# Mixing, gating and FFN pieces of a two-layer WKV/MoE kernel, put in another order on one core

## The chip, the cores and the metric

One NeuronCore of a Trainium2 chip runs the whole program; all tensors are float32. The metric is the device time of one execution in microseconds (us). The kernel before took 5168.45 us, the median of three runs (5164.87 to 5170.24). Durations below come from one profiled execution of it.

## The reference, cut to what matters

B = 4 batches, T = 1024 tokens, C = 1024 channels. `x` and the side input `f` are both (4, 1024, 1024). A bidirectional recurrence ("mixing") is run twice with other constants, for layer 0 and layer 1, on the same `f`:

```python
ek, ekv = exp(min(f, 30)), exp(min(f, 30)) * f
nf, df  = forward scans of ekv, ek along T;   nb, db = backward scans
euk     = exp(min(u + f, 30))
num, den = nf + nb - ekv + euk * f, df + db - ek + euk
mixed   = sigmoid(x) * num / max(den, 1e-8) * (0.8 + 0.2 * tf)

x = x + mixed_L0(x) @ (weight * scale[:, None]).T + bias      # layer 0
c = mixed_L1(x)                                               # layer 1, gated by the new x
x = x + moe(rmsnorm(c) * norm_w) + c     # router, top 4 of 32 experts, and a shared FFN
```

So layer 1's scans need nothing of layer 0's result; only its gate, `sigmoid(x)`, does.

## The kernel before, in words

Channels lie on the 128 partitions, eight channel tiles `ct`, and time runs along the free axis. Tokens go through TensorE in eight chunks `q` of 512 tokens, two to a batch: chunks 1 and 0 are batch 0's (the second half is done first), 2 and 3 are batch 1's, and so on.

**Mixing units.** `units` (L231) lists them as (batch, ct, layer, part). Batch 0 is cut in halves: for each layer first eight units of part 1, with both forward scans over 1024 tokens and the backward scans of the second half, and then eight *short* units of part 0, which have only the backward scans of the first half, starting from `carry`. Batches 1 to 3 have whole units, ct by ct, layer 0 and layer 1 beside each other; the two share one load of `f` and one `ek` and `ekv` (`group`, L233-235). `mixing()` (L244) is a generator that works on three units per step: `forth` of the new one (forward scans L305, ScalarE copies L306-314), `back` of the one before (exponential `euk`, L321-322, and the backward scans L325), `add_sums` of that one (two VectorE operations L352-353, a GpSimd DMA L354 that adds into `num`, and Relu, Ln and Exp on ScalarE, which make 1/den), and `quotient` (L342-348) of the one before that, whose result goes to DRAM (`c0_d` or `c1_d`, L403). In layer 0 that quotient is also multiplied by `sigmoid(x)` (`xg`, L370), with a table load before and after.

**TensorE pieces.** `first_ffn(q)` (L466) is eight pieces of 8 products with `w0t`; its first piece loads all eight `c0` tiles of the chunk and so needs all eight layer-0 units. `shared_up(q)` (L695) is 16 pieces with `wpc`, `shared_down(q)` (L722) eight. A piece takes 6.87 us. For batch 0 `first_ffn` is not gated: SyncE first copies `x` from DRAM to `resT_d` (L474), ScalarE takes the products out of PSUM (L505), and a GpSimd DMA adds them to `resT_d` (L506). `late_gate(q)` (L556) later loads `c1` and the sum back (L565-567) and `gate` (L512) computes: Sigmoid on ScalarE, the product with `c1` on VectorE (L529), Square (L530), the adding of `c1` to `resT_d` and of the square to `acc` by GpSimd DMA (L533, L537). For chunk 1 alone the squares are summed by TensorE one by one. From batch 1 on `first_ffn` is gated: `x` is loaded into SBUF (L477), VectorE takes the products out (L500), SyncE stores the sum (L501), and the gate follows two pieces later; each piece `ot` then needs layer 1's unit `ot` as well (L488).

**Normalising and routing.** After a chunk's eighth gate one product sums the squares over partitions (`ss`, L544), `norm_route` (L580) takes the root, the reciprocal (L587), scales `c1` eight times (L590), multiplies by the router (L596), and then turns rows (L607) while `shared_up` begins.

**What sets the order.** All five engines run in an order that is written out while the program is built. `run` (L441) goes through the list of pieces, keeps estimated sums of VectorE and TensorE work, and lets the mixing generator go on while VectorE's estimate is below `pace` times TensorE's; `mix_until` (L419) forces it on to a wanted unit; `after(n, f)` puts `f` n pieces later. `order()` (L957) is the list:

```python
pieces = first_ffn(FIRST, False) + first_ffn(0, False) + late_gate(FIRST)
...
pieces += shared_down(FIRST) + shared_up(0) + shared_down(0)
pieces += first_ffn(2, True) + slower(PACE[1]) + first_ffn(3, True) + shared_up(2) + shared_down(2) + shared_up(3)
```

with FIRST = 1; between the first two lines `shared_up(1)` is interleaved with `late_gate(0)`, one gate after every second piece. After batch 3's routing comes the expert part (68 pairs of blocks and 12 single ones, L1015-1172) and the last chunk's shared FFN.

Of the kernel before, what the change touches and what calls it, by code (L numbers as in the profile page):

```python
# [8 lines left out]
FP = mybir.dt.float32  # L9
I32 = mybir.dt.int32  # L10
U32 = mybir.dt.uint32
AF = mybir.ActivationFunctionType
# [10 lines left out]
P = 128  # L23
CH = 512
# [7 lines left out]
def kernel(  # L32
# [15 lines left out]
    nc = tc.nc  # L48
# [6 lines left out]
    NC = C // P  # L55
# [153 lines left out]

    W_SCANS, W_MIN, W_PASS, W_HALF = 4.7, 0.7, 1.25, 0.75  # L210
    W_PIECE, W_SMALL = 6.9, 1.0
    FIRST = 1
    LATENCY = 12.0
    PACE = 0.97, 0.9
# [14 lines left out]

    assert NCH == 2  # L230
    units = [(0, ct, L, part) for L in range(2) for part in (1, 0) for ct in range(NC)]  # L231
    units += [(b, ct, L, None) for b in range(1, B) for ct in range(NC) for L in range(2)]
    group = []  # L233
    for s, (b, ct, L, _) in enumerate(units):
        group.append(group[-1] if b > 0 and L == 1 else s - sum(1 for u in units[:s] if u[0] > 0 and u[2] == 1))
    made = set()

    def unit_of(q, ct, L):
# [5 lines left out]
    def mixing():  # L244
# [3 lines left out]
        firsts = {}  # L248
        for s in range(n):
            firsts.setdefault(group[s], s)  # L250
        ks, of, rs, xgs, kept = {}, {}, {}, {}, {}

        def columns(s):
            part = units[s][3]
# [37 lines left out]
        def forth(s, x):  # L292

            b, ct, L, part = units[s]
            dk = decay[L][:, ct, b : b + 1]
            scale = rest[L][:, ct, b : b + 1]
            if part == 0:
                of[s] = kept.pop((ct, L)), [carry[ct][:, m : m + 1] for m in range(2)]  # L300
                return
            fg = pfg.tile([P, 2, T], FP, name="fg")
            tail = pfg.tile([P, 2], FP, name="tail")
            for m in range(2):
                nc.vector.tensor_tensor_scan(fg[:, m, :], dk.to_broadcast([P, T]), x[m], 0.0, ALU.mult, ALU.add)  # L305
            nc.scalar.activation(tail, fg[:, :, T - 1], AF.Copy, scale=dk)  # L306
            if part is None:
                flat = fg.rearrange("p a t -> p (a t)")
                nc.scalar.activation(flat, flat, AF.Copy, scale=scale)
            else:  # L310
                nc.scalar.activation(fg[:, :, CH:T], fg[:, :, CH:T], AF.Copy, scale=scale)
                kept[ct, L] = places(L, ct)
                for m, to in enumerate(kept[ct, L]):
                    nc.scalar.activation(to, fg[:, m, 0:CH], AF.Copy, scale=scale)
            of[s] = [fg[:, m, columns(s)] for m in range(2)], [tail[:, m : m + 1] for m in range(2)]

        def back(s):
            b, ct, L, part = units[s]
            fg, init = of[s]

            euk = p1.tile([P, T], FP, name="ekv" if part == 0 and ct % 2 == 0 else "euk")[:, columns(s)]  # L321
            exp_ln(euk, ks[group[s]][:, columns(s)], AF.Exp, bias=v[f"u{L}"][:, ct : ct + 1])
            width = T if part is None else CH
            for m in range(2):
                nc.vector.tensor_tensor_scan(  # L325
                    fg[m][:, ::-1],
                    decay[L][:, ct, b : b + 1].to_broadcast([P, width]),
                    fg[m][:, ::-1],
                    init[m],
                    ALU.mult,  # L330
                    ALU.add,
                )
                if part == 1:
                    nc.vector.tensor_copy(carry[ct][:, m : m + 1], fg[m][:, 0:1])
            return euk

        def quotient(s):
            b, ct, L, _ = units[s]
# [8 lines left out]
            else:  # L347
                nc.vector.tensor_tensor(done, done, num, ALU.mult)

        def add_sums(s, euk):  # L350
            den, num = of[s][0]
            nc.vector.scalar_tensor_tensor(den, euk, E30, den, ALU.min, ALU.add)  # L352
            nc.vector.scalar_tensor_tensor(euk, euk, E30, ks[group[s]][:, columns(s)], ALU.min, ALU.mult)
            nc.gpsimd.dma_start(out=num, in_=euk, accum_op=ALU.add)  # L354

            r = rs[s] = p2.tile([P, T], FP, name="r")[:, columns(s)]
            nc.scalar.activation(r, den, AF.Relu, bias=ntiny)
            exp_ln(r, r, AF.Ln, bias=tiny)
            exp_ln(r, r, AF.Exp, scale=-1.0)
            if units[s][3] is None:  # L360
                fetch_x(s)
# [5 lines left out]
        for s in range(n + 2):  # L367
            new, last, old = ((u if 0 <= u < n else None) for u in (s, s - 1, s - 2))
            if old is not None and units[old][2] == 0:
                other(xgs[old], xgs[old], AF.Sigmoid)  # L370
            if last is not None and units[last][3] is not None:
                fetch_x(last)
            if new is not None:
                forth(new, (ek, ekv))
                if units[new][3] != 0:
                    yield W_SCANS
            if last is not None:
                euk = back(last)
                yield W_SCANS * share(last)
            begun = s + 1 < n and group[s + 1] != group[s]  # L380
            fresh = begun and units[s + 1][3] != 0

            early = last is not None and units[last][3] == 0
            if fresh:
                ek = begin(group[s + 1])
                yield W_MIN
            if early:
                add_sums(last, euk)
                yield 2 * W_PASS * share(last)
            if old is not None:  # L390
                quotient(old)
                yield W_PASS * (4 - units[old][2]) * share(old)
            if fresh:
                ekv = times(ek, group[s + 1])
                yield W_PASS
            if last is not None and not early:
                add_sums(last, euk)
                yield 2 * W_PASS * share(last)
            if begun:
                fetch(group[s + 1] + 1)  # L400
            if old is not None:
                b, ct, L, _ = units[old]
                nc.scalar.dma_start(out=(c0_d, c1_d)[L][b, ct, :, columns(old)], in_=rs.pop(old))  # L403
                of.pop(old)
                made.add(units[old])
# [60 lines left out]
    def first_ffn(q, gated):  # L466
# [2 lines left out]
        c0s, tiles, xs = [], {}, {}  # L469

        def early(ot):
            if not gated:

                nc.sync.dma_start(out=resT_d[ot, :, bass.ts(q, CH)], in_=xT[b, bass.ts(ot, P), cols])  # L474
            else:
                xs[ot] = px.tile([P, CH], FP, name="x")
                nc.sync.dma_start(out=xs[ot], in_=xT[b, bass.ts(ot, P), cols])  # L477
            if ot == 0:
                mix_until(*(unit_of(q, ct, 0) for ct in range(NC)))
                if q == FIRST:  # L480
                    work["tensor"] += LATENCY
                for ct in range(NC):
                    c0s.append(pc0.tile([P, CH], FP, name="c0"))
                    nc.sync.dma_start(out=c0s[ct], in_=c0_d[b, ct, :, cols])
            tiles[ot] = pw0.tile([P, NC, P], FP, name="w0t")
            nc.sync.dma_start(out=tiles[ot], in_=w0[ot])
            if gated:
                mix_until(unit_of(q, ot, 1))  # L488
                c1s[q, ot] = (ph, pc1)[q % NCH].tile([P, CH], FP, name="c1")
                nc.sync.dma_start(out=c1s[q, ot], in_=c1_d[b, ot, :, cols])  # L490
# [465 lines left out]

    def order():  # L957

        pieces = first_ffn(FIRST, False) + first_ffn(0, False) + late_gate(FIRST)

        pieces.insert(-1, Piece(lambda: None, tensor=LATENCY / 3))
        pieces += [Piece(lambda: None, tensor=0.5) for _ in range(7)]

        def slower(to):
            def do():
                pace[0] = to
                work["tensor"] = max(work["tensor"], work["vector"] / to)

            return [Piece(do, tensor=0.0)]

        pieces += slower(PACE[0])
        up, gates = shared_up(FIRST), late_gate(0)
        for i, piece in enumerate(up):
            pieces.append(piece)
            if i % 2 == 1:
                pieces.append(gates.pop(0))
        pieces += gates
        pieces += shared_down(FIRST) + shared_up(0) + shared_down(0)
        pieces += first_ffn(2, True) + slower(PACE[1]) + first_ffn(3, True) + shared_up(2) + shared_down(2) + shared_up(3)
        for b in range(2, B):  # L980
            q = NCH * b
            pieces += first_ffn(q, True) + first_ffn(q + 1, True) + shared_down(q - 1)
            pieces += shared_up(q) + shared_down(q)
            if b + 1 < B:
                pieces += shared_up(q + 1)
        return pieces
# [472 lines left out]
```

## Time and profile before

| What | Value |
|---|---|
| Median of three runs | 5168.45 us |
| The profiled execution, whole | 5166.87 us |
| Its span, first to last instruction | 5165.1 us |
| TensorE busy | 4844.4 us, 94% |
| VectorE busy | 3151.5 us, 61% |
| First product | at 140.54 us |
| First product of chunk 0 / of `shared_up(1)` | at 236.28 / 367.24 us |
| First product of `first_ffn(2)` / of `shared_up(2)` | at 775.21 / 905.89 us |

How to read it: the page gives each engine's busy time and, in 40 slices of 129 us, its busy tenths. The view of waits tells which instruction of an engine stood idle before it ran and what ended that. The timeline lists instructions with start, duration, and, in brackets, the idle time before them with its releaser. "PE" is TensorE, "DVE" VectorE, "ACT" ScalarE, "POOL" GpSimd, "SP" SyncE; a name such as "ACTq" is the DMA issue of that engine. Each float32 product is recorded twice, so a piece of 8 products is x16.

### The profile page before, as it was taken

The page shows a single profiled execution, that of the slowest core. Times are in us where ns is not written, and L with a number is a line of the kernel's source. Part 1 is how long each engine was busy: PE and PEld are TensorE (multiplying, and loading weights), DVE is VectorE, ACT ScalarE, POOL GpSimd, SP SyncE. Part 2 cuts the span into 40 slices and gives each one's busy share as a digit, 9 for nine tenths or more (in the row PEclk, how much of TensorE's full clock was granted, in tenths as well). Part 3 has the DMA queues.
Part 4 walks back from the last instruction along what each step waited for, and adds up shares of the span by engine and source line. Part 5 has one row for each costly group of instructions (what it writes and reads, how often), then busy time and mean ns, then how long its engine had stood idle before and what let it go on. Part 6 is the DMA issues. An engine that isn't in the chain of part 4 may idle for free.

```text
span 5165.1 us, 36964 instructions
## 1 busy us (share of the span) xinstructions
PE 4844.4 (94%) x12906; PEld 2241.6 (43%) x12906; DVE 3151.5 (61%) x3432; ACT 1504.7 (29%) x1972; POOL 821.5 (16%) x781
## 2 busy tenths in 40 slices
PE   0668989999999999999999999999999999999999
PEld 0223434444444444444444444444444444444444
DVE  8777999797780221665665656565656566565621
ACT  6666666656561120111111111111111111111110
POOL 1112201311220120111111111111111111111110
PEclk9879999999999999999999999999999999999999
DMA  4776769669754855577777676767777777767684
GB/s 139 205 183 173 194 181 304 169 181 274 210 163 120 247 149 197 177 217 236 221 227 239 210 246 204 250 204 241 215 233 220 231 237 215 241 216 238 214 233 123
DMA packets 532279, 1081.99 MB, mean 209 GB/s; under 512 B 31538, under 2 KB 261043, under 8 KB 531475
## 3 DMA queue, kind: packets, MB, share of 16 engines
q1 hardware_dynamic: 386338, 744.70, 42.5%
q0 software_dynamic: 76960, 223.13, 20.7%
q10 hardware_dynamic: 68784, 111.69, 6.3%
q8 instruction: 105, 1.72, 0.1%
q14 instruction: 92, 0.75, 0.0%
HBM read 848.33 MB, written 203.56 MB: 204 GB/s over the span
## 4 chain that ended last, share of the span: by engine, by line
PE 59%; ACT 0%; issue 0%; DVE 0%; ACTq 0%
PE gA L1182 14%; PE gC L1182 9%; PE gB L1182 9%; PE dA L1182 7%; PE dB L1182 5%; PE dC L1182 5%; PE tr L1036 2%; PE gA L1070 2%; PE gB L1070 2%; PE tr L1119 1%; PE dA L1132 1%; PE dB L1132 1%; PE dA L1370 0%; PE gC L1370 0%; PE gA L1370 0%; PE gB L1370 0%
## 5 line engine op out<-in xcount | busy, mean ns | idle before, releaser
L707 PE MATMUL mm<-c,wpc 128*128 128x512 f32 x1792 | 785.5, 598 | 11.9 <-ACT sact L225 9.4
L495 PE MATMUL mm<-c,w0t 128*128 128x512 f32 x1024 | 455.4, 606 | 195.0 <-DMA w0t<-in_w 182.9
L707 PEld LDWEIGHTS mm<-c,wpc 128*128 128x128 f32 x1792 | 340.7, 192 | 432.4 <-issue 416.1
L1182 PE MATMUL gA<-w,hsT 128*128 128x512 f32 x1088 | 489.7, 593 | 0.0
L1182 PE MATMUL gB<-t_up,s_up 128*128 128x512 f32 x1088 | 489.1, 592 | 0.0
L1182 PE MATMUL gC<-w,s_up 128*128 128x512 f32 x1088 | 489.1, 592 | 0.0
L1166 POOL DMA_INDIRECT sum_d<-y,tokens x148 | 303.2, 2049 | 920.1 <-DMA sum_d<-y,tokens 540.4
L735 PE MATMUL mm<-sact,wpc 128*128 128x512 f32 x896 | 397.7, 599 | 9.3 <-DVE sact L716 9.3
L933 POOL DMA_INDIRECT hs<-h_d,tokens x146 | 147.4, 1009 | 1623.7 <-PE tr L1036 1552.1
L495 PEld LDWEIGHTS mm<-c,w0t 128*128 128x128 f32 x1024 | 198.5, 195 | 448.3 <-issue 419.7
L1182 PEld LDWEIGHTS gC<-w,s_up 128*128 128x128 f32 x1088 | 206.7, 190 | 260.2 <-issue 260.2
L1182 PEld LDWEIGHTS gB<-t_up,s_up 128*128 128x128 f32 x1088 | 206.7, 190 | 260.2 <-issue 244.4
L900 DVE TENSOR_TENSOR t_up<-w,w 128x2048 f32<-128x2048 f32 x136 | 310.7, 2284 | 0.0
L1182 PEld LDWEIGHTS gA<-w,hsT 128*128 128x128 f32 x1088 | 201.7, 190 | 227.9 <-issue 227.9
L325 DVE TENSOR_TENSOR_SCAN fg<-decay,tail,fg 128x1024 f32<-128x1024 f32 (+1 forms) x128 | 260.2, 2064 | 0.0
L735 PEld LDWEIGHTS mm<-sact,wpc 128*128 128x128 f32 x896 | 169.2, 193 | 209.1 <-issue 197.6
L1037 ACT COPY hsT<-tr 128x512 f32<-128x512 f32 x296 | 172.7, 588 | 292.5 <-PE tr L1036 292.5
L1182 PE MATMUL dB<-t_down,s_down 128*128 128x512 f32 x544 | 256.9, 594 | 0.1
L1182 PE MATMUL dA<-w,actT 128*128 128x512 f32 x544 | 255.8, 592 | 0.0
L1182 PE MATMUL dC<-w,s_down 128*128 128x512 f32 x544 | 255.8, 592 | 0.0
L1107 ACT ACTIVATE act<-c 128x512 f32<-128x512 f32 x68 | 42.8, 630 | 708.9 <-DVE c L1103 708.9
L1182 PE MATMUL gA<-t_up,hsT 128*128 128x512 f32 x544 | 244.5, 592 | 0.0
(272 smaller groups left out, 6343.1 us busy)
## 6 DMA issues: line engine op xcount, KB each, us to landing
w<-in_w SPq DMA_DIRECT2D x240, 2048.0 KB
c<-c_d SPq DMA_DIRECT2D x128, 256.0 KB
w0t<-in_w SPq DMA_DIRECT2D x64, 512.0 KB
wpc<-in_sg SPq DMA_DIRECT2D x56, 512.0 KB
wpc<-in_su SPq DMA_DIRECT2D x56, 512.0 KB
wpc<-in_sd SPq DMA_DIRECT2D x56, 512.0 KB
fg<-euk POOLq DMA_DIRECT2D x48, 512.0 KB
c_d<-r ACTq DMA_DIRECT2D x48, 512.0 KB
```

Of the source, the lines that this page charges most:

```text
L325: nc.vector.tensor_tensor_scan(fg[m][:, ::-1], decay[L][:, ct, b : b + 1].to_broadcast([P, width]), fg[m][:, ::-1], init[m], ALU.mult, ALU ...
L495: nc.tensor.matmul(mm, lhsT=tiles[ot][:, it, :], rhs=c0s[it], start=(it == 0), stop=(it == NC - 1))
L707: nc.tensor.matmul(mm, lhsT=wts[f, n][:, kt, :], rhs=c1s[q, kt], start=(kt == 0), stop=(kt == NC - 1))
L735: nc.tensor.matmul(mm, lhsT=wts[ct][:, f, :], rhs=acts[q, f], start=(f == 0), stop=(f == NSI - 1))
L900: nc.vector.tensor_tensor(to, x, y, ALU.subtract)
L933: nc.gpsimd.indirect_dma_start(out=to, out_offset=None, in_=h_d, in_offset=bass.IndirectOffsetOnAxis(ap=have["tokens"][:, i, n : n + 1], a ...
L1036: nc.tensor.transpose(tr[:, r, :], hs[:, bass.ts(4 * q + r, P)], ident)
L1037: nc.scalar.copy(self.hsT[:, 4 * q : 4 * q + 4, b, :], tr)
L1070: nc.tensor.matmul(ps, lhsT=self.hsT[:, k, 0, :], rhs=w[k // NK][:, k % NK, bass.ts(n, I)], start=(k == 0), stop=(k == NC - 1),)
L1132: nc.tensor.matmul(ps, lhsT=self.actT[:, k, 0, :], rhs=w[:, k, bass.ts(n, 512)], start=(k == 0), stop=(k == NI - 1),)
L1166: nc.gpsimd.indirect_dma_start(out=sum_d, out_offset=bass.IndirectOffsetOnAxis(ap=tokens[:, i, self.n : self.n + 1], axis=0), in_=y, in_of ...
L1182: nc.tensor.matmul(ps, lhsT=x[:, k, :], rhs=w[:, k, :], start=(k == 0 and not more), stop=(k == half - 1), skip_group_check=more,)
```

## The change

Five edits, all in the first third of the program:

- The exponential `euk` of a short unit is computed in `forth`, one step earlier than in `back`; three buffers take turns for it (`ekv`, `euk`, `ek`).
- The copy of `x` to `resT_d` is issued by GpSimd from the mixing loop, one copy of 1024 tokens per channel tile of batches 0 and 1 (16 copies), and no longer by SyncE (16 copies of 512 tokens for batch 0).
- In batch 1 layer 0 of channel tiles 5, 6 and 7 is mixed ahead of layer 1 of these tiles. The two layers of a tile are then not neighbours, so that these three load `f` and compute `ek` and `ekv` a second time.
- `late_gate(1)` is spread between the pieces of `first_ffn(0)`: its first two pieces (the first load and gate 0) after the fourth, gate 1 after the sixth, gate 2 after the eighth, the rest behind.
- Batch 1 becomes ungated like batch 0: `first_ffn(2)` with nothing between, `late_gate(2)` between the pieces of `first_ffn(3)` (its last gate behind them), eight empty pieces, and `late_gate(3)` between the pieces of `shared_up(2)`.

```diff
-    units += [(b, ct, L, None) for b in range(1, B) for ct in range(NC) for L in range(2)]
+    SOON = 5
+    units += [(1, ct, L, None) for ct in range(SOON) for L in range(2)]
+    units += [(1, ct, L, None) for L in range(2) for ct in range(SOON, NC)]
+    units += [(b, ct, L, None) for b in range(2, B) for ct in range(NC) for L in range(2)]
...
             if part == 0:
+                euks[s] = bonus(s)
...
+        def bonus(s):
+
+            _, ct, L, part = units[s]
+
+            euk = p1.tile([P, T], FP, name=("ekv", "euk", "ek")[ct % 3] if part == 0 else "euk")[:, columns(s)]
+            exp_ln(euk, ks[group[s]][:, columns(s)], AF.Exp, bias=v[f"u{L}"][:, ct : ct + 1])
+            return euk
...
-            euk = p1.tile([P, T], FP, name="ekv" if part == 0 and ct % 2 == 0 else "euk")[:, columns(s)]
-            exp_ln(euk, ks[group[s]][:, columns(s)], AF.Exp, bias=v[f"u{L}"][:, ct : ct + 1])
+            if part != 0:
+                euks[s] = bonus(s)
...
+            if new is not None:
+                b, ct, L, part = units[new]
+                if b < LATE and L == 0 and part != 0:
+
+                    nc.gpsimd.dma_start(out=resT_d[ct, :, bass.ts(b, T)], in_=xT[b, bass.ts(ct, P), :])
...
-            if not gated:
-
-                nc.sync.dma_start(out=resT_d[ot, :, bass.ts(q, CH)], in_=xT[b, bass.ts(ot, P), cols])
-            else:
+            if gated:
...
-        pieces = first_ffn(FIRST, False) + first_ffn(0, False) + late_gate(FIRST)
+        pieces = first_ffn(FIRST, False)
+        pieces += woven(first_ffn(0, False), late_gate(FIRST), (4, 4, 6, 8))
...
         pieces += shared_down(FIRST) + shared_up(0) + shared_down(0)
-        pieces += first_ffn(2, True) + slower(PACE[1]) + first_ffn(3, True) + shared_up(2) + shared_down(2) + shared_up(3)
+        pieces += first_ffn(2, False)
+        pieces += woven(first_ffn(3, False), late_gate(2), (0, 1, 2, 3, 4, 5, 6, 7, 8)[1:])
+        pieces += [Piece(lambda: None, tensor=0.5) for _ in range(8)]
+        pieces += slower(PACE[1])
+        pieces += woven(shared_up(2), late_gate(3), tuple(range(2, 17, 2)))
+        pieces += shared_down(2) + shared_up(3)
```

`woven(pieces, others, at)` puts one of `others` behind piece number `at[0]`, then the next behind `at[1]`, and so on, and what is left at the end. LATE is 2.

## The prediction

> **What bounds the kernel now.** I read the page first, for where TensorE idles, then TensorE's waits over the whole span, then its timeline at the longest waits, and last VectorE's and ScalarE's rows there. The page:
>
> ```profile
> span 5165.1 us, 36964 instructions
> ...
> PE 4844.4 (94%) x12906; PEld 2241.6 (43%) x12906; DVE 3151.5 (61%) x3432; ACT 1504.7 (29%) x1972; POOL 821.5 (16%) x781
> ...
> PE   0668989999999999999999999999999999999999
> ...
> DVE  8777999797780221665665656565656566565621
> ```
>
> TensorE is the bound, and its 320.7 us of idle time lie in the first slices, where VectorE's mixing feeds it. Its waits, with total, number and longest:
>
> ```profile
> PE mm L495 <- DMA w0t<-in_w: 182.9, 7, 140.5
> PE ss L544 <- ACT y L530: 40.3, 7, 18.0
> PE tr L740 <- DVE rT L749: 15.0, 2, 13.6
> PE mm L495 <- ACT x L505: 12.1, 2, 8.9
> ```
>
> Of the 182.9, 140.5 is the start. The others in the timeline, each row with its start, duration and, in brackets, the idle time before it:
>
> ```profile
> 193.26 8.74 PE L495 MATMUL mm<-c,w0t 128*128 128x512 f32 x16 [8.91 <-ACT x L505]
> ...
> 236.28 57.46 PE L495 MATMUL mm<-c,w0t 128*128 128x512 f32 x128 [23.97 <-DMA w0t<-in_w]
> 311.70 2.05 PE L544 MATMUL ss<-y,ones 128*128 128x512 f32 x2 [17.95 <-ACT y L530]
> ...
> 768.80 1.08 PE L740 MATMUL tr<-ident,rT 128*128 128x128 f32 x4 [13.62 <-DVE rT L749]
> 775.21 9.60 PE L495 MATMUL mm<-c,w0t 128*128 128x512 f32 x16 [5.32 <-DMA w0t<-in_w]
> ```
>
> Between the first product and 1600 us some 148 us are idle: 12 in `first_ffn(1)`, 24 before chunk 0, 47 in the gates of chunk 1, 21 in `shared_up(1)` and the start of `shared_down(1)`, 19 before `first_ffn(2)`, 7 in it, and rests. That is all this change can touch. From 905.89 to 1195 there is no idle time.
>
> **Short units (A).** A short unit's rows show why chunk 0 is late:
>
> ```profile
> 161.36 1.26 DVE L325 TENSOR_TENSOR_SCAN c<-decay,carry,c 128x512 f32<-128x512 f32 x1
> 164.64 0.69 DVE L352 SCALAR_TENSOR_TENSOR sact<-ekv,sact 128x512 f32<-128x512 f32 x1 [2.02 <-ACT ekv L221]
> ```
>
> ```profile
> 187.64 1.28 ACT L220 ACT_TABLE_LOAD   x1 [7.76 <-DMA resT_d<-in_xT]
> ```
>
> VectorE needs 6.6 us a unit (two scans of 1.2, two sums of 0.7, a quotient of 2.85) but repeats every 8.65, since ScalarE does two table loads and the sigmoid before `euk`. Between 124.4 and 226.9 VectorE waits 25.5 us for that exponential, 7.8 of them because ScalarE's DMA issue at 179.9 stood behind an `x` copy of SyncE. With `euk` a step earlier, ScalarE bounds the unit: two table loads (1.30 from start to next start), sigmoid 0.64, exp 0.73, the three functions of 1/den 2.13, some 0.5 for the DMA issue and its wait: 6.6, and 7.0 with half an eviction of L505. Eight times 8.65 - 7.0 is 13, the lost `x` copy wait 8, less one where a buffer's add DMA holds the exponential on ScalarE and with it the 1/den queued behind: **-20 us** for the first product of chunk 0 (236.3 to 216). The cover is thin: ScalarE has no slack left in such a unit. The Trainium skill ("ScalarE: Activation LUTs", What ACT_TABLE_LOAD costs) speaks against this gain: a switch costs 1.28 us plus a drain of about 1.38. By that the unit would take 7.0 + 2.8 = 9.8 us (an estimate), and the edit would gain nothing. The row has the load at 1.28, the next function starts 1.30 after it, and the whole unit repeats in 8.65; the sum goes by the row.
>
> **`x` copied by GpSimd.** Sixteen issues; GpSimd's rows for the same kind of transfer (L354) are 0.84 to 1.21 us, so 13 to 19 us on an engine 16% busy. In its queue a copy stands behind the unit's own add DMA, and the next add comes 13 us later; who would wait is `quotient`. DMA share is 0.46 in the first 100 us. Bounds: -8 (the wait counted in A) to +3 us (a small one as in `r L345 <- DMA fg<-euk`, 1.4, twice); I take 0 beyond A. The trace has no such copy from GpSimd. The Trainium skill ("SBUF — State Buffer", SBUF: two separate sides) warns that VectorE's two-port operations keep GpSimd from writing descriptors, 620 ns becoming about 3100; by that, 16 copies would cost GpSimd 40 us more (an estimate). L354's issues, median 0.86 us with VectorE 94% busy around many of them, show no such thing.
>
> **Gates between products (B).** By the instruction order only gates 0 and 1 move ahead of VectorE's last part-1 unit, and one `ss` ahead of the last piece; six gates stay behind. From 305.9 to 351.8 VectorE works 27 of 46 us and ScalarE 38, with table loads on both sides of each gate. Two of eight gates leave that stretch, and its first waits (1.2 + 5.1 + 1.3) go with them: **-8 us** on top of A, so `shared_up(1)` starts at 367.2 - 28 = 339. If ScalarE, now fuller, merely shifts the wait, 0; at best all nine waits of the stretch go, -17.
>
> **The second set of short units (C).** Layer 1's short units make VectorE wait 8.4 us for `euk` after 390. TensorE idles 21 us in `shared_up(1)` and before `shared_down(1)` because VectorE lags there: **-8 us**, bounds 0 and -15.
>
> **Three channels' c0 ahead (D).** In the instruction order two layer-1 units (tiles 5 and 6) leave VectorE's stretch ahead of the last layer-0 unit of batch 1: four scans of 2.2, two sums of 1.2 and a quotient of 3.6 are 15 each, 30 us. The three repeated `ek` and `ekv`, 1.7 each, come later and are in E's sum; their loads of 512 KB wait on a queue that ran two units ahead. The 13.6 + 5.3 us before `first_ffn(2)` are late mixing and **-19** goes; `x` and `c1` are no longer loaded in that stretch (DMA share 1.03 at 782 to 880), so I take **-5** of the 7.1 us inside it, bounds 0 and -7. `first_ffn(3)` then ends near 898.9 - 60 = 839.
>
> **Batch 1's gates, late (E).** This is the price. Before, chunk 2's normalisation ran under `first_ffn(3)`: its reciprocal stands at 879.98, and `shared_up(2)` started without a wait. After, in the order of the instructions, gates 6 and 7 and all of `norm_route` stand behind the last product of `first_ffn(3)`, with eight pieces that contain nothing. VectorE still has, from the last L749 of `shared_down(0)` (one piece after `first_ffn(2)` begins at 775 - 28 - 8 - 19 = 720: 727) to gate 7: 26 scans of 2.2, 24 quotient operations of 1.25, 12 sums of 1.2, 3 `ek` and `ekv` of 1.7, 8 gates of 0.65, together 112 us. From 782.5 to 880 it was busy 86.9 of 97.5 (89%), so 126: gate 7 at 853. Then product and square 1.4; two adds into `acc`, which must follow one another (GpSimd waits 22.9 us on `acc<-y` from 782 to 905, and the units' adds L354 queue behind it), 4.9 each (an add of this size: issued 115.45, waited for until 120.38): 9.8; `ss` 0.8; and from the end of `ss` to the first product, as at chunk 1 (349.7 to 367.2), 17.5. Sum 29.5: `shared_up(2)` starts at 882.5, some 43 us after the last product, instead of 7. Against 905.9 the gain is down to 23. Bounds for these 43: 25 (VectorE without a wait, adds of 2.5) to 104 (VectorE 60% busy, as from 305.9 to 351.8).
>
> **After that (F).** `late_gate(3)` lies between the pieces of `shared_up(2)` as `late_gate(0)` did, where 21 us were lost; here VectorE has whole units and more slack (its rows reach each piece's product some 12 us ahead, against 6 there), and ScalarE has 16 evictions of 0.67 more, VectorE 16 fewer L500. I take **+3**, bounds 0 and +15. Later pieces and the experts are as before.
>
> Sum: -23 + 3 = -20 from the profiled execution's 5166.87 (span 5165.1): 5147. That execution lies 1.6 us under the median of 5168.45, well inside the three runs' 5 us, so I keep 5147.
>
> **Rivals.**
> *E eats it all: slower.* Place: TensorE's idle time behind `first_ffn(3)`. Mechanism: the gates stand in VectorE's queue between whole units of batch 2, and each unit waits on ScalarE and GpSimd. From 305.9 to 351.8, where gates and units alternate, VectorE worked only 60%. At 65% the 112 us take 172, gate 7 falls at 899, `shared_up(2)` at 928.5: +23, with F 5193. It decides from `shared_up(2)` later than 903, that is VectorE below 76% there. Against it: 89% in the stretch with gates of before.
> *ScalarE takes the exponential's place: no change.* If a short unit still takes 8 us, A is -6 and B -4; VectorE arrives everywhere 18 later than I say, `shared_up(2)` starts at 900.5, and 5164 results. For it: ScalarE's sum of 7.0 is within 0.4 of VectorE's.
> *The chain is hidden: faster still.* If VectorE's waits of 54 us between 390 and 775 shrink by 20 more and adds land in 2.5, `shared_up(2)` starts at 858: 5122.
> *It doesn't do what it says*: half true of B, as counted above.
>
> **How the numbers follow.** Forecast near 5147 (5132 to 5157): 0.46. Hidden chain, 5105 to 5132: 0.22. No change, 5157 to 5178: 0.19. Slower, 5178 to 5205: 0.13. A measurement of this kernel can tell some 0.2%, 10.3 us, from no change; faster means below 5158: 0.46 + 0.22 + 0.02 = 0.70; same 0.17; slower 0.13. The range leaves out 0.13 above and some 0.05 below: 5110 to 5176.
>
> **What would show it.** A: chunk 0's first product near 216, no waits of 2.02 on `euk`. B: `shared_up(1)` near 339. D: no 13.6 us wait at L740. E: an idle time of about 40 us ahead of L544 and L596 after `first_ffn(3)`. F: few waits at L707 in `shared_up(2)`. The forecast is wrong if E's idle time passes 60 us or A's waits stay.

## The result, and the profile after

The changed kernel takes 5162.26 us (median of 12 runs, 5158.6 to 5172.95); the kernel before took 5168.9 in its 12 runs. The medians differ by 6.6 us; the ratio over all runs is 0.9991 [0.9982, 1.0000], which is 4.7 us. The two profiled executions, 5166.87 and 5162.16, differ by 4.7 as well, and the stages below are theirs. Forecast were 20. All these differences lie within the 0.2% that a measurement can hardly tell from no change.

The page of the changed kernel:

```profile
span 5160.4 us, 37011 instructions
...
PE 4841.1 (94%) x12906; PEld 2239.3 (43%) x12906; DVE 3146.0 (61%) x3422; ACT 1518.4 (29%) x1991; POOL 855.4 (17%) x813
...
PE   0768996999999999999999999999999999999999
```

TensorE's first slices are fuller than before (7 for 6 in the second, 9 for 8 in the sixth), but the seventh, 774 to 903 us, has fallen from 9 to 6. TensorE's waits, with total, number and longest, tell what is in it:

```profile
PE mm L510 <- DMA w0t<-in_w: 154.3, 3, 142.5
PE ss L559 <- ACT y L545: 34.5, 7, 12.1
PE ss L559 <- DMA acc<-y: 33.9, 1, 33.9
```

The third line is new. Beyond the start (142.5), `mm` waits 11.8 us for loads and, in the timeline below, 19.4 more before chunk 0; before, it waited 42.4 for loads beyond the start and 12.1 for ScalarE. One sum of squares now waits 34. TensorE's timeline of the kernel before, where nothing waits between the last pieces of `first_ffn(3)` and `shared_up(2)`:

```profile
878.21 20.76 PE L495 MATMUL mm<-c,w0t 128*128 128x512 f32 x48
898.91 7.05 PE L596 MATMUL tr<-c,rw_sb 128*32 128x512 f32 x16
905.89 7.13 PE L707 MATMUL mm<-c,wpc 128*128 128x512 f32 x16
```

and of the changed kernel:

```profile
219.30 51.34 PE L510 MATMUL mm<-c,w0t 128*128 128x512 f32 x112 [19.43 <-issue]
...
731.83 7.03 PE L510 MATMUL mm<-c,w0t 128*128 128x512 f32 x16
...
791.10 56.87 PE L510 MATMUL mm<-c,w0t 128*128 128x512 f32 x128 [3.29 <-DMA w0t<-in_w]
881.91 2.08 PE L559 MATMUL ss<-acc,ones 128*128 128x512 f32 x2 [33.95 <-DMA acc<-y]
889.03 9.70 PE L611 MATMUL tr<-c,rw_sb 128*32 128x512 f32 x16 [5.04 <-DVE c L605]
...
900.69 7.03 PE L722 MATMUL mm<-c,wpc 128*128 128x512 f32 x16
```

`first_ffn(3)` ends at 847.97, 51 us earlier than before; `shared_up(2)` starts at 900.69, 5 earlier. TensorE has no product of a piece for 52.7 us in between. The same in stages, each from TensorE's first product of one part to that of the next:

| Stage | before | after | change | forecast |
|---|---|---|---|---|
| start to the first product | 140.54 | 142.49 | +1.9 | 0 |
| to chunk 0 | 95.74 | 76.81 | -18.9 | -20 (A) |
| to `shared_up(1)` | 130.96 | 125.63 | -5.3 | -8 (B) |
| to `first_ffn(2)` | 407.97 | 386.90 | -21.1 | -27 (C, D) |
| to `first_ffn(3)` | 65.66 | 59.27 | -6.4 | -5 (D) |
| to `shared_up(2)` | 65.02 | 109.59 | +44.6 | +36.6 (E) |
| to `first_ffn(4)` | 295.24 | 302.10 | +6.9 | +3 (F) |
| to the end | 3964.0 | 3957.6 | -6.4 | 0 |
| sum | 5165.1 | 5160.4 | -4.7 | -20.4 |

VectorE's waits of the changed kernel from 740 to 885:

```profile
DVE acc L602 <- ACT acc L226: 13.2, 1, 13.2
DVE c L544 <- ACT y L226: 11.9, 3, 6.3
```

The first is the chain behind gate 7; the second is gates waiting for their sigmoid. Gate 7 runs at 870.79, and the chain of 29.9 us follows, up to 900.69: two adds into `acc` one after the other, the sum of squares, the reciprocal, the scaling and the router.

```profile
870.79 0.75 DVE L544 SCALAR_TENSOR_TENSOR c<-c,nosc,y 128x512 f32<-128x512 f32 x1 [1.31 <-ACT y L226]
```

```profile
873.07 0.86 POOL L552 DMA_DIRECT2D acc<-y  x1 [1.27 <-DMA acc<-y]
...
878.56 0.86 POOL L552 DMA_DIRECT2D acc<-y  x1 [3.75 <-DMA acc<-y]
```

```profile
884.75 3.35 DVE L602 RECIPROCAL acc<-acc 128x512 f32<-128x512 f32 x1 [13.21 <-ACT acc L226]
```

### The profile page after: what moved, and what is told of

It reads as the page before. It is cut to its first block, busy times and chain, and to the rows that moved or that the text cites. A ratio compares the mean times of both kernels' runs of the same rounds, so it can differ in the third digit from the quotient of the medians.

```text
span 5160.4 us, 37011 instructions
## 1 busy us (share of the span) xinstructions
PE 4841.1 (94%) x12906; PEld 2239.3 (43%) x12906; DVE 3146.0 (61%) x3422; ACT 1518.4 (29%) x1991; POOL 855.4 (17%) x813
## 4 chain that ended last, share of the span: by engine, by line
PE 59%; ACT 0%; issue 0%; DVE 0%; ACTq 0%
PE gA L1208 14%; PE gC L1208 9%; PE gB L1208 9%; PE dA L1208 7%; PE dB L1208 5%; PE dC L1208 5%; PE tr L1062 2%; PE gA L1096 2%; PE gB L1096 2%; PE tr L1145 1%; PE dA L1158 1%; PE dB L1158 1%; PE gA L1396 0%; PE dA L1396 0%; PE gC L1396 0%; PE gB L1396 0%
## 5 line engine op out<-in xcount | busy, mean ns | idle before, releaser
L1208 PEld LDWEIGHTS gA<-w,hsT 128*128 128x128 f32 x1088 | 201.7, 190 | 227.9 <-issue 227.9
```

The costliest lines, as they stand in the source:

```text
L1208: nc.tensor.matmul(ps, lhsT=x[:, k, :], rhs=w[:, k, :], start=(k == 0 and not more), stop=(k == half - 1), skip_group_check=more,)
```

## The experiments

**Theory.** Four edits bring VectorE some 51 us ahead, and the fifth, batch 1's late gates, spends it: the gates and `norm_route` of chunk 2 stand behind the last product of `first_ffn(3)` and have nothing to cover them. **Rivals:** VectorE's mixing sets `shared_up(2)` wherever the gates are; or an added cost (GpSimd's copies, the repeated `ek` and `ekv`) uses the gain up.

Ratios are to runs of the kernel before on the same chip, and so are the gains and losses of whole runs given below. Runs e1 to e4, e5 to e8 and e9 to e12 were on three chips, where the kernel before took 5170.5, 5174.4 and 5168.4; runs from different groups are better compared by their ratios than by their medians. The last column is from one profiled execution each, in us from its start.

| Run | median us | ratio to before | first products: chunk 0, `first_ffn(2)`, `(3)`, `shared_up(2)`, `first_ffn(4)` |
|---|---|---|---|
| e1 gates as before | 5135.76 | 0.9932 [0.9915, 0.9948] | 220.7, 733.2, 811.5, 877.2, 1174.2 |
| e2 gates early | 5170.06 | 0.9999 [0.9989, 1.0008] | 219.7, 730.1, 810.8, 896.9, 1206.6 |
| e3 batch 2 held | 5162.82 | 0.9984 [0.9974, 0.9993] | 220.7, 736.0, 795.0, 885.8, 1203.3 |
| e4 both | 5168.96 | 0.9995 [0.9985, 1.0004] | 219.4, 736.5, 814.5, 896.5, 1210.3 |
| e5 as e1, c1 later | 5116.23 | 0.9887 [0.9871, 0.9904] | 221.6, 735.4, 801.3, 866.6, 1161.9 |
| e6 as e1, D undone | 5144.44 | 0.9942 [0.9925, 0.9958] | 220.7, 748.0, 814.5, 879.4, 1174.6 |
| e7 before + late gates | 5216.21 | 1.0082 [1.0065, 1.0099] | 238.6, 778.8, 838.9, 948.0, 1251.2 |
| e8 before + exponential | 5149.90 | 0.9954 [0.9938, 0.9971] | 227.9, 760.5, 825.6, 890.5, 1185.7 |
| e9 after, x by SyncE | 5169.73 | 1.0003 [0.9994, 1.0013] | 227.0, 744.2, 806.1, 916.1, 1218.6 |
| e10 as e5, B undone | 5118.37 | 0.9903 [0.9886, 0.9919] | 218.1, 733.9, 800.7, 865.6, 1160.9 |
| e11 as e5, x by SyncE | 5118.72 | 0.9906 [0.9889, 0.9922] | 219.8, 733.5, 801.1, 867.1, 1162.3 |
| e12 as e5, all c1 later | 5114.68 | 0.9897 [0.9881, 0.9914] | 219.0, 733.5, 800.4, 866.1, 1161.4 |

**Batch 1's gates as before.** `LATE = 1` also leaves out GpSimd's eight copies of `x` for batch 1, which gates as before do not use.

```diff
-    LATE = 2
+    LATE = 1
-        pieces += first_ffn(2, False)
-        pieces += woven(first_ffn(3, False), late_gate(2), (0, 1, 2, 3, 4, 5, 6, 7, 8)[1:])
-        pieces += [Piece(lambda: None, tensor=0.5) for _ in range(8)]
-        pieces += slower(PACE[1])
-        pieces += woven(shared_up(2), late_gate(3), tuple(range(2, 17, 2)))
+        pieces += first_ffn(2, True) + slower(PACE[1]) + first_ffn(3, True) + shared_up(2)
```

> The changed kernel with batch 1 gated as before: its two first_ffn chunks are gated piece by piece, x is loaded into SBUF, and no late gates; the other four edits stay. My theory: the early edits brought 43 to 51 us up to the end of first_ffn(3) (847.97 against 898.9) and batch 1's late gates gave back all but 5 of them, in the idle time of 53 us ahead of shared_up(2). With gates as before, the 130.7 us that lay between the first product of first_ffn(2) and that of shared_up(2) follow the 731.8 of the changed kernel: shared_up(2) near 865, the whole near 5130 (5122 to 5140). Rival, VectorE's backlog: whatever the placing of the gates, VectorE has not finished the mixing and scaling that shared_up(2) needs, and it starts at 890 to 900: 5150 to 5162. Second rival, added cost elsewhere (copies by GpSimd, repeated ek and ekv): no better than the changed kernel, 5160.

The kernel takes 5136, 35 us less than before where the changed one took 5 less. The theory holds, though 6 us short of its number, and a new wait stands where the shortfall is. TensorE's timeline of this run:

```profile
811.46 37.38 PE L510 MATMUL mm<-c,w0t 128*128 128x512 f32 x80 [22.25 <-DMA w0t<-in_w]
...
877.21 3.27 PE L722 MATMUL mm<-c,wpc 128*128 128x512 f32 x7
```

and SyncE's DMA issues there:

```profile
768.64 0.33 SPq L501 DMA_DIRECT2D w0t<-in_w  x1
790.55 0.33 SPq L505 DMA_DIRECT2D c<-c_d  x1
...
792.76 5.25 SPq L499 DMA_DIRECT2D c<-c_d  x8
```

SyncE's waits from 740 to 860 show what held it:

```profile
SPq L505 <- DMA c_d<-r: 23.8, 2, 21.5
```

From 768.97 SyncE stood at a load of `c1` (L505) whose unit had not been written out yet, and the eight `c0` loads of chunk 3 (L499), whose units were all done before `first_ffn(2)` began, stood behind it in the same queue.

**The c1 loads of batch 1 two pieces later** (on top of the last run).

```diff
-            if gated:
-                mix_until(unit_of(q, ot, 1))
-                c1s[q, ot] = (ph, pc1)[q % NCH].tile([P, CH], FP, name="c1")
-                nc.sync.dma_start(out=c1s[q, ot], in_=c1_d[b, ot, :, cols])
+            if gated:
+                if b != 1:
+                    load_c1(ot)
...
         def do(ot):
+            if gated and b == 1:
+                load_c1(ot)
```

`load_c1` holds the three lines taken out.

> As the run with gates as before, and in batch 1 the load of c1 is issued two pieces later, so that on SyncE the eight c0 loads of chunk 3 stand ahead of the last two c1 loads. In the run with gates as before SyncE stood from 768.97 to 790.55 at the load of tile 7's c1, whose layer-1 unit is now mixed last, and TensorE waited 22.25 us at first_ffn(3). My theory: the third edit's price is this queue; without it first_ffn(3) starts at 792 and the whole takes 5136 - 18 = 5118 (5112 to 5124). Rival: VectorE is that late anyway, the wait moves to a product that waits for L515 or to the scaling ahead of shared_up(2): 5132 to 5138.

5116, 58 us under before: the queue was the cause of most of the wait. TensorE's timeline:

```profile
801.32 36.91 PE L516 MATMUL mm<-c,w0t 128*128 128x512 f32 x80 [9.96 <-DMA w0t<-in_w]
...
866.60 7.13 PE L728 MATMUL mm<-c,wpc 128*128 128x512 f32 x16
```

The wait of 22 is down to 10, and no other wait took its place: VectorE was not the limit, and that rival falls for gates as before. What the last 10 us wait for was not tried. Of the 17.2 us between the two profiled spans, 12.3 are there at `first_ffn(4)`; the other 4.9 come behind it and are not explained.

**The late gates alone**, on the kernel before (`x` is copied by SyncE); the helper `woven` is the change's.

```diff
-        pieces += first_ffn(2, True) + slower(PACE[1]) + first_ffn(3, True) + shared_up(2) + shared_down(2) + shared_up(3)
+        pieces += first_ffn(2, False)
+        pieces += woven(first_ffn(3, False), late_gate(2), (0, 1, 2, 3, 4, 5, 6, 7, 8)[1:])
+        pieces += [Piece(lambda: None, tensor=0.5) for _ in range(8)]
+        pieces += slower(PACE[1])
+        pieces += woven(shared_up(2), late_gate(3), tuple(range(2, 17, 2)))
+        pieces += shared_down(2) + shared_up(3)
```

> The kernel before with nothing but batch 1's gates late (first_ffn(2) and (3) ungated, late_gate(2) between the pieces of first_ffn(3), late_gate(3) in shared_up(2); x copied by SyncE). My theory: this edit costs what it cost in the changed kernel: VectorE reaches gate 7 some 131 us after the last L749 (782.5), at 913, shared_up(2) 29 later at 943 instead of 906, and 7 more behind it: 5203 (5190 to 5210). Rival: the edit is harmless, and the changed kernel is held back by its other edits: 5165 to 5175.

Slower by 42 us, and in the place expected:

```profile
929.27 2.08 PE L544 MATMUL ss<-acc,ones 128*128 128x512 f32 x2 [29.94 <-DMA acc<-y]
...
947.97 2.31 PE L707 MATMUL mm<-c,wpc 128*128 128x512 f32 x5
```

From the first product of `first_ffn(3)` to that of `shared_up(2)` it takes 109.1 us here, 109.6 in the changed kernel, 65.0 before. The loss in this stage is the same with and without the other edits. On the whole it is 42 us here and some 30 on top of the four others (the ratios of e1 and the changed kernel): there the gates as before bring the wait of 22 at `first_ffn(3)`, which late gates do not have (3.3), so the two sums do not simply add up to the change. The 5203 of the expectation was added wrongly: 37 and 7 on 5166.9 are 5211, and 5215.63 is the profiled execution.

**Could late gates be had for less?** Three variants of the changed kernel: the gates of chunk 2 from the fourth piece of `first_ffn(2)` on (e2); mixing withheld from `first_ffn(3)` to the last gate, so that no unit of batch 2 stands between the gates on VectorE (e3); both (e4).

```diff
-        pieces += first_ffn(2, False)
-        pieces += woven(first_ffn(3, False), late_gate(2), (0, 1, 2, 3, 4, 5, 6, 7, 8)[1:])
+        pieces += woven(first_ffn(2, False) + first_ffn(3, False), late_gate(2), (4, 4, 5, 6, 7, 8, 9, 10, 11))
```

```diff
-            while work["vector"] < pace[0] * work["tensor"] and mix():
+            while not held[0] and work["vector"] < pace[0] * work["tensor"] and mix():
...
         pieces += first_ffn(2, False)
+        pieces += hold(True)
         pieces += woven(first_ffn(3, False), late_gate(2), (0, 1, 2, 3, 4, 5, 6, 7, 8)[1:])
         pieces += [Piece(lambda: None, tensor=0.5) for _ in range(8)]
+        pieces += hold(False)
```

`hold` sets the flag and raises VectorE's estimate to `pace` times TensorE's.

> The changed kernel with batch 1's first eight late gates seven or so pieces earlier: they start behind the fourth piece of first_ffn(2), one after each piece, and the last stands behind the third piece of first_ffn(3). The mixing between them is not touched. If the order of the gates alone makes the idle time (the chain of sigmoid, product, square, adds and sum behind the last product), the chain now runs under the products, and shared_up(2) starts 17.5 us after 848, near 866: 5126. If it is what stands on VectorE ahead of the reciprocal (some 100 of the 131 us between 740 and 871 are units of batch 2, which nobody needs before 1200), VectorE reaches the reciprocal only some 15 us earlier, near 868 instead of 884.75, and shared_up(2) starts near 885: 5144. If neither, 5160.

> The changed kernel with the mixing of batch 2 held back from the first piece of first_ffn(3) until the last gate of chunk 2 has been written out; the gates stay where they are. If VectorE's units of batch 2 are what delays the gates: the last gate then waits only for the eviction of the last product on ScalarE (near 849), and the chain of 29 from there gives shared_up(2) near 879 instead of 900.7: 5139. If the order of the gates alone makes the idle time, nothing: 5158 to 5162. If batch 2's mixing is missed later, first_ffn(4) starts with a wait, and the time is 5160 or more.

> Both: batch 1's first eight late gates as early as in the run with early gates, and batch 2's mixing held back from the first piece of first_ffn(3) until they are written out. If VectorE's queue and the gates' place each hold a part, both go: the sum of squares stands at the last product, and shared_up(2) starts 17.5 us behind 848, near 866: 5126 (5120 to 5135). If batch 2's mixing is then too late for first_ffn(4) (its last layer-0 unit was done some 70 us ahead of need), 10 to 20 us come back there: 5140. If VectorE's necessary work sets it, as in the run with early gates: 5144.

None gains anything clear over the changed kernel: e2 and e4 missed every number given for them, and e3 ended in the last of its three cases. Behind `first_ffn(3)` each did part of what it should: TensorE's stretch without products fell from 52.7 us to 29 (e2), 34 (e3) and 24 (e4). So some 19 of the 52.7 went with the units of batch 2 that stand between the gates, and 34 stayed without them. Each paid elsewhere. With early gates SyncE waits again, for the sums that the gates load (L582 loads `resT_d` for a late gate), with chunk 3's `c0` behind. SyncE's waits of e2 from 740 to 860:

```profile
SPq L582 <- DMA resT_d<-x: 46.5, 6, 16.1
```

so that `first_ffn(3)` starts 20 us later than in the changed kernel. With batch 2 held, the mixing left undone is missed later: in e3 VectorE waits for eight sigmoids while it has nothing else (its waits from 740 to 870),

```profile
DVE c L545 <- ACT y L226: 48.8, 8, 12.2
```

and 317 instead of 302 us pass between `shared_up(2)` and `first_ffn(4)`, which starts late:

```profile
1203.26 57.85 PE L511 MATMUL mm<-c,w0t 128*128 128x512 f32 x128 [11.30 <-DMA w0t<-in_w]
```

All seven units that VectorE begins between 735 and 848 in the changed kernel are batch 2's (the forward scan of `ek` at 735.5 is its 33rd, after 16 for batch 0 and 16 for batch 1), and the prediction did not see that nobody needs them before 1200. They were no idle filler all the same: put off as a block, as in e3, they are late there.

**Three channels' c0 not ahead** (on top of e1).

```diff
-    SOON = 5
+    SOON = NC
```

> As the run with gates as before, and batch 1's units in the order of before, layer 0 and layer 1 of each tile beside each other (the third channel edit undone). If that edit gains at the start of first_ffn(2) what it gives back at first_ffn(3) through the c1 load, first_ffn(2) starts 15 to 20 us later, near 750, first_ffn(3) without the wait of 22, and the time is the same: 5132 to 5140. If the edit is a clear gain: 5148 to 5156.

5144, between the two. `first_ffn(2)` starts 14.8 us later, with the old waits of 13.9 and 5.1 before it, but the wait of 22 shrinks to 7.7, and `shared_up(2)` is only 2 us later than in e1:

```profile
747.99 9.85 PE L510 MATMUL mm<-c,w0t 128*128 128x512 f32 x16 [5.11 <-DMA w0t<-in_w]
...
814.50 36.48 PE L510 MATMUL mm<-c,w0t 128*128 128x512 f32 x80 [7.71 <-DMA w0t<-in_w]
```

With the c1 loads in their old place the edit is used up by the queue. What e1 still has over e6 comes behind 1174: 9 us in the two profiles, 5 by the two ratios, whose intervals overlap. The edit with the c1 loads moved was not tried by itself.

**The exponential ahead, alone** on the kernel before; the helper `bonus` is the change's.

```diff
             if part == 0:
+                euks[s] = bonus(s)
...
+            if part != 0:
+                euks[s] = bonus(s)
```

> The kernel before with nothing but the exponential of the short units one step ahead (x copied by SyncE as before). My theory: chunk 0's first product moves from 236 to 220 to 225, the second set of short units gains some more in shared_up(1), VectorE stays ahead by that up to shared_up(2), and most arrives at the end: 5150 (5145 to 5157). Rival: the gain is used up at the gates of chunk 1, where ScalarE is as full as before: 5162 to 5168.

5150, as expected: `first_ffn(2)` and `shared_up(2)` are both 15 us earlier, so A and C pass on whole where no late gates follow. Chunk 0's first product moves only to 227.9.

**Who copies x.** In the changed kernel (e9) and on top of e5 (e11) GpSimd's copies are taken out and SyncE's put back.

```diff
-                    nc.gpsimd.dma_start(out=resT_d[ct, :, bass.ts(b, T)], in_=xT[b, bass.ts(ct, P), :])
...
+            if not gated:
+                nc.sync.dma_start(out=resT_d[ot, :, bass.ts(q, CH)], in_=xT[b, bass.ts(ot, P), cols])
```

> The changed kernel with x copied by SyncE again, 512 tokens at a time, and no copies by GpSimd. The prediction gave the copies by GpSimd nothing but the 8 us of ScalarE's wait behind an x copy. If that is right, chunk 0's first product goes from 219.3 back to 226 to 228, where the run with the exponential alone had it (227.88), the first product from 142.5 back to 140.5, and the whole is 5 to 8 us longer than the changed kernel: 5167 to 5171. Rival: the copies by GpSimd crowd the first stage (DMA share there 0.57 against 0.48) and cost as much as they bring: 5160 to 5164.

> As the run with c1 later (5116), with batch 0's x copied by SyncE again. By my theory VectorE's lead at the first short units goes through to the end where no late gates of batch 1 take it back, so the copies by GpSimd are worth 5 to 8 here too: 5121 to 5124. Rival: no difference, 5116.

e9 has chunk 0 at 227.0 and is some 6 us over the changed kernel by the two ratios, whose intervals overlap. (Its profiled execution, 5177.5, was the slowest of ten, so the later columns of its row overstate the loss.) e11, with the same first stage, has chunk 0 at 219.8, as early as with GpSimd's copies; its ratio is 0.9906 to e5's 0.9887, whose intervals overlap too. The main difference between these two profiles is one load: in e9 VectorE waited 8.9 us for the first `f` of layer 1 and 5.5 for the add DMA behind it, in e11 5.6 and 1.4. The copies are worth something between 0 and 10 us; this does not settle it.

**Chunk 1's gates behind the products again** (on top of e5).

```diff
-        pieces += woven(first_ffn(0, False), late_gate(FIRST), (4, 4, 6, 8))
+        pieces += first_ffn(0, False) + late_gate(FIRST)
```

> As the run with c1 later (5116), with all gates of chunk 1 behind the products of chunk 0 again. The prediction gave this edit 8 us. From the traces (first product of chunk 0 to that of shared_up(1): 130.0 with the exponential alone, 126.4 with the gates between) it is worth 3.6: 5120 (5117 to 5122). If it is worth its 8: 5124. Rival: later slack of VectorE takes it all, 5116.

130.0 us instead of 126.8 from chunk 0 to `shared_up(1)`, so the edit is worth 3.2 there. But `first_ffn(2)` begins at 733.9, and at 735.4 in e5: nothing of it is left at that point in these two profiles, as the rival had it. The ratios, 0.9903 and 0.9887, have overlapping intervals, so a gain of a few us on the whole is neither shown nor excluded.

**All c1 loads later** (e5's edit for batches 2 and 3 too).

```diff
-            if gated:
-                if b != 1:
-                    load_c1(ot)
...
-            if gated and b == 1:
+            if gated:
                 load_c1(ot)
```

> As the run with c1 later (5116), with the c1 load two pieces later in batches 2 and 3 as well. TensorE waits 7.58 us at first_ffn(5) and 1.49 at first_ffn(7) in that run. If SyncE's place of the c1 loads is behind these waits too: 4 to 6 us less, 5111. If they come from the c0 buffers (the last c0 tiles of a chunk can load only when the last piece before has begun): 5115 to 5118.

No difference from e5 that can be told (the intervals overlap), and `first_ffn(5)` still waits 7.6: there the queue is not the cause. That it is the `c0` buffers was only argued.

## Why the prediction was right or wrong

**What bounds it, and where the loss lies:** right. E's idle time stands in the place named; it was forecast at 43 and is 52.7, above the forecast but under the 60 us that the prediction had named as a sign of being wrong, and A's waits are gone. So neither of its own signs showed, and the gain was still a quarter of the forecast: terms were mis-sized, E most of all.

**A (-20; measured -18.9):** the sum held, two of its reasons did not, so that its closeness is partly luck. Starts of successive short units' scans in the changed kernel:

```profile
132.24 1.28 DVE L338 TENSOR_TENSOR_SCAN sact<-decay,carry,sact 128x512 f32<-128x512 f32 x1
...
138.84 1.28 DVE L338 TENSOR_TENSOR_SCAN sact<-decay,carry,sact 128x512 f32<-128x512 f32 x1
...
173.25 0.69 DVE L275 TENSOR_SCALAR ek<-k 128x1024 f32<-128x1024 f32 x1 [5.33 <-DMA k<-in_fT]
```

A unit repeats in 6.60 us: VectorE's own work, not ScalarE's 7.0. But the 8 us "behind an `x` copy" did not go: without SyncE's copies ScalarE's table load still waits as long, now by the profile for a `w0t` load.

```profile
186.26 1.28 ACT L226 ACT_TABLE_LOAD   x1 [8.39 <-DMA w0t<-in_w]
```

VectorE is by then so far ahead that it does not wait for the exponential behind this load, but for `f` (5.33). In e12, whose first stage is the changed kernel's, the same load waits 7.93 and the profile names a scan of VectorE; with SyncE's copies put back it waits 4.47 (e11) and 1.24 (e9). What it waits for stays open, but the wait does not need those copies. How the 18.9 divide stays open: the exponential alone brought chunk 0 forward by 8.4 (e8), with the other edits but without GpSimd's copies by 9.3 (e9) and 16.5 (e11). By the prediction's estimate from the Trainium skill ("ScalarE: Activation LUTs", What ACT_TABLE_LOAD costs), with a drain of 1.38 behind each switch, the unit would have taken 9.8 us. This case shows 6.60, so the drain is not paid here.

**`x` copied by GpSimd (0):** about right. L418 took 0.86 us in the median, 16 times; the delay to 3.1 us that the Trainium skill ("SBUF — State Buffer", SBUF: two separate sides) warns of is not there; whether any VectorE operation here is of the two-port kind that it speaks of, no run shows. Unforeseen were 2 us at the first product: 142.5 to 144.2 in all runs with these copies, 140.3 to 141.7 without. DMA share before 140 us rose from 0.48 to 0.56; that this is the reason was not tried.

**B (-8; -5.3) and C, D (-27; -21.1):** right in kind, too large. B was to take 7.6 us off TensorE's waits for the squares of chunk 1; all its waits of this sort fell from 40.3 to 34.5, one of them still 12.1, and e10 puts the edit at 3.2. C is 5.4 of its 8 (e8), D 14.1 of its 19 (e6 against e1): the waits of 13.9 and 5.1 in e6 are gone in e1, but one of 4.3 at 680, in `shared_down(0)`, came; that the three channels' layer-0 units crowd VectorE earlier is the likely reason, not tried.

**E (+36.6; +44.6): the step that failed.** "126, so gate 7 at 853" was 131 from the last L749 (L764 in the changed kernel), which itself came 13 us later than forecast, at 739.9. The work (112 us) was right, VectorE's 89% was not: with gates after every piece it also waits for their sigmoids (11.9 us) and worked 111.8 of 130.9 us, 85%. The chain of 29.5 us was 29.9. And the step had no allowance for what leads it: what A to D fall short and the start adds, 12 us in all up to 731.83, moves gate 7 back by as much. E, named at 36.6, cost 44.6 in its stage; e7 finds the same 44 without the other edits.

**F (+3; +6.9), and the end (0; -6.4):** F was too low but within its bounds. The gain behind 1202 was not foreseen, and it was luck: TensorE's waits for ScalarE's evictions between 1349 and 1421 (7.2 us, the longest 4.6) are gone, and `first_ffn(5)` waits 8.5 instead of 4.2. That stage took 3954 to 3960 us in the ten profiles with three channels' c0 ahead and 3961 to 3968 in the four without, so it seems to go with the units' order, though by less than a microsecond between the two groups; why was not tried.

**Rivals.** The time came out where "no change" had it (5164), by another way: short units at 6.6 us, and the loss in E's stretch. "E eats it all" named the mechanism and put its edge at 903; it stopped 2 us short of it. The whole is a difference of two large sums: before E -60 forecast and -50 measured, for E and F +40 and +51. Errors of a sixth in the one and three tenths in the other leave nothing of the 20: by themselves these stages come to +1.7. The 4.7 us that the profiles do show come from the 6.4 behind 1202, which were not forecast.

## What to carry to other kernels

When an edit takes work off the path early and puts a chain without cover behind it, forecast and test the two by themselves: here four edits were worth 35 us (58 with one queue cleared) and the fifth cost 42 by itself and some 30 on top of them, and only undoing one part at a time showed it. Of a chain that ends behind the last product, whatever has no other products beside it is lost: 52.7 us in the changed kernel, and still 24 to 34 in the three variants that started it earlier or cleared its way. And when a load waits for data that are produced late, look at what stands behind it in the same queue: issuing one batch's `c1` loads two pieces later was worth some 20 us, 12 of them at the wait itself.

## What was not expected of the hardware

- ScalarE's wait of 8.4 us at a table load stayed when the copy it was put down to was gone; the profile then names another load (`w0t`). In e12 it names a scan of VectorE for the same wait (7.93). A releaser that only stands in time beside the end of a wait need not be its cause.
- Adding 256 KB into `acc` by GpSimd's DMA, one after another: the last two were issued at 873.07 and 878.56, the second after a wait of 3.75 on the first, and the sum of squares started 3.4 us after the second issue: 3.4 to 5.5 us each, one behind the other.
